# The last two steps of a graph network kernel's layer 3: products combined, weighed, normalized and stored one by one, with row additions on GpSimd

## The chip, the cores and the metric

The kernel runs on one core of a Trainium2 chip. A core has a matrix engine (TensorE, PE in the profile, with its weight loads as PEld), VectorE (DVE), ScalarE (ACT), GpSimd (POOL) and SyncE (SP, which here only issues transfers). They run at the same time, each in its own instruction order, and wait for one another by semaphores. The metric is the device time of one execution in microseconds.

## The reference

Four layers over 4096 nodes with 256 features, each followed by a residual addition and a layer normalization. Layer 0 is a masked attention with four heads, layer 1 a graph attention, and layers 2 and 3 are graph convolutions. The change concerns the end of layer 3:

```python
def _L3_gnn_ref(H, A_tilde, W):
    d_inv_sqrt = jnp.sum(A_tilde, axis=1) ** (-0.5)
    A_norm = d_inv_sqrt[:, None] * A_tilde * d_inv_sqrt[None, :]
    H_next = A_norm @ H @ W
    return jax.nn.relu(H_next)
...
# x: (4096, 256), adj: (4096, 4096)
x = _layernorm(x + _L0_gnn_ref(x, adj, adj, ...), axis=-1)
x = _layernorm(x + _L1_gnn_ref(x, adj, L1_gnn_W, L1_gnn_a), axis=-1)
x = _layernorm(x + _L2_gnn_ref(x, adj, L2_gnn_W, L2_gnn_b), axis=-1)
x = _layernorm(x + _L3_gnn_ref(x, adj, L3_gnn_W), axis=-1)
return x
```

## The kernel before, in words

Everything is float32. Layers 0 and 1 come first and are not touched. Layers 2 and 3 share one loop of 128 steps, 64 a layer (`n_all = 2 * T1`). A layer computes adj @ y, where y is x scaled by the inverse root of the row sums, in four blocks (`jb`) of output nodes. A block covers 512 nodes of the first half of the nodes and the 512 at the same place in the second half, and runs over 16 steps (`c`), each with one chunk of 128 input nodes from either half.

The 2x2 split of nodes and features lets a step use seven products in place of eight (Strassen's scheme). `sums` (L946) makes five sums and differences of the adjacency chunk on VectorE, `prepare` (L910) made those of y earlier, and `Block.product` (L959) issues product i of step t: one matmul of 128x128 with 128x512 that accumulates over the block's 16 steps in PSUM tile `m[i]`. [...]

When a block ends, `keep` (L982) copies the seven results to the SBUF tile `e`, four on ScalarE (L986) and three on VectorE (L988). `combine(h)` (L991) adds them up on VectorE into `hT`, the transposed result of half h. `rows(n)` (L1007) handles one chunk of 128 output nodes, n from 0 to 7: two matmuls with the layer's weights into `py` (L1014), for layer 3 a relu with scale on ScalarE (L1028) into a tile `relu` that has three buffers, an addition onto the residual `xc` on VectorE (L1029), and the statistics of the row (`ln_stats`, L115 and L116). `block_rstd` (L903) turns the eight variances into inverse deviations (L906 to L908), and `store(h)` (L1032) normalizes four chunks into `ob` on VectorE (`ln_apply`, L124) and sends them to `out` by one transfer of 512 KB from SP (L1037).

The order is written by hand (`tc.manual_schedule`): each engine gets its instructions in program order. For every block but the last, `at_step` (L1043) spreads these later parts over the following steps, so that they lie beside the next block's products. For the last block there is no next one: after the last step the loop breaks and everything runs in sequence, with the rows' `py` in the PSUM tiles of the products:

```python
            for h in range(2):
                blk.combine(h)
                for n in range(h * NSJ, (h + 1) * NSJ):
                    blk.rows(n, f"m{n % 7}")
            block_rstd(NJB - 1)
            for h in range(2):
                blk.store(h)
```

`load` (L935) fetches the adjacency three steps ahead on SP; `sums(t + 1)` stands ahead of the products of step t.

Of the kernel before, what the change touches and what calls it, by code (L numbers as in the profile page):

```python
# [8 lines left out]
F32 = mybir.dt.float32  # L9
BF16 = mybir.dt.bfloat16  # L10
AF = mybir.ActivationFunctionType
ALU = mybir.AluOpType
# [4 lines left out]
P = 128  # L17
N = 4096
D = 256
# [5 lines left out]
BJ = 512  # L25
# [19 lines left out]
def tile_gnn(  # L45
# [18 lines left out]
    nc = tc.nc  # L64
# [18 lines left out]
    d3 = const.tile([P, NCH], F32, name="d3")  # L83
# [8 lines left out]
    xc = keep.tile([P, NCH, D], F32, name="xc")  # L92
# [20 lines left out]
    def ln_stats(pool, row, ci):  # L113
        st = pool.tile([P, 6], F32, tag="bnst", name="bnst")
        nc.vector.bn_stats(st, row)  # L115
        nc.vector.bn_aggr(mv[:, ci, :], st)  # L116

    def ln_rstd(c0, c1):
        nc.vector.tensor_scalar(rstd[:, c0:c1], mv[:, c0:c1, 1], EPS, None, ALU.add)
        nc.scalar.activation(rstd[:, c0:c1], rstd[:, c0:c1], AF.Sqrt)  # L120
        nc.vector.reciprocal(rstd[:, c0:c1], rstd[:, c0:c1])

    def ln_apply(dst, src, ci):
        nc.vector.tensor_scalar(  # L124
            dst, src, mv[:, ci, 0:1], rstd[:, ci : ci + 1], ALU.subtract, ALU.mult
        )

# [43 lines left out]
    with ExitStack() as l0:  # L171
# [6 lines left out]
        wk = l0.enter_context(tc.tile_pool(name="l0work", bufs=1))  # L178
# [176 lines left out]
        class Pair:  # L355
# [80 lines left out]
            def sums(self):  # L436

                u = 2 * self.rows.ib + self.pr
                l2 = wk2.tile([P, 2], F32, tag="l2", name="l2")
                nc.vector.tensor_reduce(l2, self.ls, AX.X, ALU.add)  # L440
                nc.vector.reciprocal(l2, l2)

                lt = wk2.tile([P, QB], F32, tag="lt", name="lt")
                nc.vector.transpose(lt, l2.unsqueeze(1).to_broadcast([P, QB // 2, 2]))
                for j in range(2):
                    nc.gpsimd.dma_start(
                        norm[u, j, :].rearrange("(a c) -> a c", c=QB),
                        lt.rearrange("(a r) c -> a r c", r=QB)[:, j, :],
                    )
# [17 lines left out]
        rows = [Rows(ib) for ib in range(NCH)]  # L467
# [244 lines left out]
    with ExitStack() as l1:  # L712
        wk = l1.enter_context(tc.tile_pool(name="l1work", bufs=2))
# [166 lines left out]
    with ExitStack() as l2:  # L880
# [3 lines left out]
        wk = l2.enter_context(tc.tile_pool(name="l2work", bufs=3))  # L884
        ps_m = l2.enter_context(tc.tile_pool(name="l2ps_m", bufs=1, space=PSUM))

        w2_sb = big.tile([P, 2, D], F32, name="w2_sb")
# [3 lines left out]
        w3_sb = big.tile([P, 2, D], F32, name="w3_sb")  # L891
        nc.scalar.dma_start(w3_sb, w3.rearrange("(c p) e -> p c e", p=P))

        NP = NCH // 2
        NJB = N // 2 // BJ
        NSJ = BJ // P
        T1 = NJB * NP
        y = store[:, 0 : 2 * NP * D].rearrange("p (h c e) -> p h c e", h=2, c=NP)
# [4 lines left out]
        def block_rstd(jb):  # L903
            cs = slice(jb * NSJ, (jb + 1) * NSJ)
            r = rstd2[:, :, cs]
            nc.vector.tensor_scalar(r, mv2[:, :, cs, 1], EPS, None, ALU.add)  # L906
            nc.scalar.activation(r, r, AF.Sqrt)
            nc.vector.reciprocal(r, r)  # L908

        def prepare(p, layer):  # L910

            dv = d2 if layer == 0 else d3
            for h in range(2):
                ci = h * NP + p
                ln_apply(xc[:, ci, :], xc[:, ci, :], ci)
                nc.scalar.activation(
                    y[:, h, p, :], xc[:, ci, :], AF.Copy, scale=dv[:, ci : ci + 1]
                )
                if layer == 0:
                    nc.gpsimd.tensor_tensor(xc[:, ci, :], xc[:, ci, :], b2_b, ALU.add)  # L920
            s = ysum[:, p, :, :]
            nc.vector.tensor_tensor(
                s[:, 1:3, :].rearrange("p a d -> p (a d)"), y[:, 0, p, :], y[:, 1, p, :], ALU.subtract
            )
            nc.vector.tensor_tensor(
                s[:, 3:5, :], y[:, :, p, 0:P], y[:, :, p, P : 2 * P], ALU.add
            )
            nc.vector.tensor_tensor(
                s[:, 0, :], y[:, 0, p, 0:P], y[:, 1, p, P : 2 * P], ALU.add
            )  # L930
# [23 lines left out]
        class Block:  # L954
# [49 lines left out]
                    tt(o, o, e[2], ALU.add)  # L1004
                    tt(o, o, e[5], ALU.subtract)

            def rows(self, n, tag="y"):  # L1007

                h, s = divmod(n, NSJ)
                ci = h * NP + self.jb * NSJ + s  # L1010
                w = w2_sb if self.layer == 0 else w3_sb
                py = ps_m.tile([P, 512], F32, tag=tag, name="py")
                for f in range(2):
                    nc.tensor.matmul(  # L1014
                        py[:, 0:D],
                        self.hT[:, h, f, s * P : (s + 1) * P],
                        w[:, f, :],
                        start=(f == 0),
                        stop=(f == 1),
                    )  # L1020
                row = xc[:, ci, :]
                if self.layer == 0:
                    nc.vector.scalar_tensor_tensor(
                        row, py[:, 0:D], d2[:, ci : ci + 1], row, ALU.mult, ALU.add
                    )
                else:
                    r = wk.tile([P, D], F32, tag="relu", name="relu")
                    nc.scalar.activation(r, py[:, 0:D], AF.Relu, scale=d3[:, ci : ci + 1])  # L1028
                    nc.vector.tensor_tensor(row, row, r, ALU.add)  # L1029
                ln_stats(wk, row, ci)  # L1030

            def store(self, h):  # L1032
                ob = wk.tile([P, NSJ, D], F32, tag="ob", name="ob", bufs=2)
                c0 = h * NP + self.jb * NSJ
                for s in range(NSJ):
                    ln_apply(ob[:, s, :], xc[:, c0 + s, :], c0 + s)
                nc.sync.dma_start(  # L1037
                    out[c0 * P : (c0 + NSJ) * P, :].rearrange("(s p) e -> p s e", p=P), ob
                )
# [3 lines left out]
        def at_step(t, when, f, *args):  # L1043
            later.setdefault((t, when), []).append((f, args))

        def do(t, when):
            for f, args in later.pop((t, when), []):
                f(*args)

        n_all = 2 * T1  # L1050
# [3 lines left out]
        with tc.manual_schedule():  # L1054
            prepare(0, 0)
            sums(0)
            prepare(1, 0)
            blk = None
            for t in range(n_all):
                layer, tl = divmod(t, T1)  # L1060
                jb, c = divmod(tl, NP)
                if c == 0:
                    blk = Block(layer, jb)
                if t + 3 < n_all:
                    load(t + 3)
                if t + 1 < n_all:
                    sums(t + 1)
                for i in range(7):
                    blk.product(i, t)
                    if i == 2:  # L1070
                        do(t, "mid")
                del adj_t[t], adj_s[t]
                if layer == 0 and jb == 0 and c + 2 < NP:
                    prepare(c + 2, 0)
                do(t, "end")
                if c == NP - 1:
                    blk.keep()
                    if t == n_all - 1:
                        break
                    at_step(t + 1, "mid", blk.combine, 0)  # L1080
                    at_step(t + 2, "mid", blk.combine, 1)
                    for n in range(2 * NSJ):
                        at_step(t + 2 + n // 2, ("mid", "end")[n % 2], blk.rows, n)
                    at_step(t + 2 + NSJ, "mid", block_rstd, jb)
                    for s in range(NSJ):
                        p = jb * NSJ + s
                        if layer == 0:

                            free = (NJB - 1) * NP + p + NSJ + 2
                            at_step(max(t + 2 + NSJ + s, free), "end", prepare, p, 1)  # L1090
                    if layer == 1:
                        for h in range(2):
                            at_step(t + 3 + NSJ + h, "end", blk.store, h)
            for h in range(2):
                blk.combine(h)
                for n in range(h * NSJ, (h + 1) * NSJ):
                    blk.rows(n, f"m{n % 7}")
            block_rstd(NJB - 1)
            for h in range(2):
                blk.store(h)  # L1100


# [49 lines left out]
```

## Time and profile before

| | us |
|---|---|
| median of 3 runs (2745.74 to 2746.96) | 2745.95 |
| the profiled execution | 2743.03 |
| its span, first to last instruction | 2741.3 |
| last two steps start (products) | 2703.33 |
| last product ends, about | 2715.4 |
| last normalization ends, about | 2736.9 |

The profile's times count from the span's start. Two rows of the groups show what the same kind of addition takes on two engines (columns: line, engine, operation, output and inputs with shapes, count, then busy us and the mean ns of one, then idle time before it):

```profile
L1029 DVE TENSOR_TENSOR xc<-xc,relu 128x256 f32<-128x256 f32 x8 | 3.3, 409 | 4.3 <-ACT relu L1028 4.3
...
L920 POOL TENSOR_TENSOR xc<-xc,b_b 128x256 f32<-128x256 f32 x32 | 25.5, 816 | 529.1 <-ACT store L916 529.1
```

The first row is the last block's additions. The second is the only addition of this size that GpSimd does in these two layers, at the start of layer 2. A duration in such a row is from an instruction's start to its end; neighbours on one engine may overlap a little.

### The profile page before, as it was taken

The numbers are of one execution on the slowest core, as the hardware profiler recorded it, in microseconds if no ns is written. First come the engines' busy times: TensorE is split into PE (matmuls) and PEld (weight loads), VectorE is DVE, ScalarE is ACT, GpSimd is POOL, SyncE is SP. The second block draws the span as 40 slices with busy tenths as digits, with TensorE's granted clock in tenths as the row PEclk, the third lists the DMA queues.
The fourth block names the chain that finished last, engine by engine and source line by source line (L and its number), as shares of the span: only waits on it lengthen the run. The fifth ranks groups of instructions, "written<-read, shape, count | busy, mean of one in ns | idle before, by whom it ended". The sixth has DMA issues, their size and how long they took to land.

```text
span 2741.3 us, 58184 instructions
## 1 busy us (share of the span) xinstructions
PE 2688.6 (98%) x23440; PEld 1840.8 (67%) x23440; DVE 2183.8 (80%) x3995; ACT 1648.0 (60%) x2675; POOL 379.4 (14%) x660
## 2 busy tenths in 40 slices
PE   8999999999999999999979999999999999999997
PEld 5777777777777777777768888886444444444443
DVE  4899889899898989889758888885866578666565
ACT  2899999999999999999857777771100001000000
POOL 1232222232222222222200000001200000000000
PEclk9999999999999999999999999999999999999998
DMA  6444444444444444444352222203545544555552
GB/s 148 94 94 95 89 92 95 90 92 92 91 95 91 91 94 95 86 95 95 125 171 77 77 77 77 73 28 118 178 158 164 167 160 154 169 173 165 184 170 75
DMA packets 679486, 312.31 MB, mean 114 GB/s; under 512 B 553520, under 2 KB 583600, under 8 KB 679216
## 3 DMA queue, kind: packets, MB, share of 16 engines
q1 hardware_dynamic: 655776, 265.10, 38.9%
q0 software_dynamic: 21632, 42.05, 4.3%
q8 instruction: 183, 3.00, 0.5%
q10 hardware_dynamic: 1808, 1.44, 0.2%
q14 instruction: 87, 0.71, 0.1%
HBM read 262.41 MB, written 46.07 MB: 113 GB/s over the span
## 4 chain that ended last, share of the span: by engine, by line
PE 96%; DVE 2%; issue 1%; DMA 1%; ACT 1%; SPq 0%; POOL 0%; DVEq 0%; ACTq 0%; POOLq 0%
PE m L980 27%; PE po L428 18%; PE sc L371 16%; PE po L802 16%; PE ptr L410 11%; PE py L1014 2%; PE pp L340 1%; PE pq L319 1%; PE pv L232 1%; PE pk L212 1%; PE sc L139 1%; DMA xt<-in_xT 0%; SPq L262 0%; DMA rb<-norm 0%; DVE pt L416 0%
## 5 line engine op out<-in xcount | busy, mean ns | idle before, releaser
L380 DVE CUSTOM_DVE_ANT_0 z<-sc,bias 128x1024 f32<-128x1024 f32 x512 | 606.0, 1221 | 48.0 <-PE sc L371 47.9
L396 ACT ACTIVATE z<-z,nm 128x1024 f32<-128x1024 f32 x512 | 590.4, 1153 | 0.0
L418 ACT COPY pt<-ptr 128x1024 f32<-128x1024 f32 x507 | 510.5, 1007 | 78.3 <-PE ptr L410 75.2
L428 PE MATMUL po<-pt,xc 128*64 128x128 f32 x8192 | 504.1, 276 | 0.0
L371 PE MATMUL sc<-store,qT 64*128 64x512 f32 x2048 | 502.9, 604 | 0.1
L802 PE MATMUL po<-store,pt 128*128 128x257 f32 x2048 | 447.6, 380 | 12.6 <-issue 12.6
L428 PEld LDWEIGHTS po<-pt,xc 128*64 128x64 f32 x8192 | 442.1, 137 | 17.5 <-DVE pt L416 0.2
L410 PEld LDWEIGHTS ptr<-ident,z 64*128 64x128 f32 x8192 | 322.0, 138 | 178.4 <-issue 82.5
L802 PEld LDWEIGHTS po<-store,pt 128*128 128x128 f32 x2048 | 388.9, 190 | 71.1 <-issue 12.7
L980 PE MATMUL m<-asum,ysum 128*128 128x512 f32 x768 | 356.2, 593 | 6.3 <-issue 6.3
L410 PE MATMUL ptr<-ident,z 64*128 64x64 f32 x8192 | 356.6, 225 | 4.5 <-ACT pt L418 3.2
L371 PEld LDWEIGHTS sc<-store,qT 64*128 64x128 f32 x2048 | 192.7, 188 | 116.7 <-issue 109.8
L980 PEld LDWEIGHTS m<-asum,ysum 128*128 128x128 f32 x768 | 146.0, 190 | 177.9 <-issue 161.2
L980 PE MATMUL m<-asum,store 128*128 128x512 f32 x512 | 262.3, 594 | 0.0
L980 PE MATMUL m<-a,ysum 128*128 128x512 f32 x512 | 245.7, 593 | 0.0
L986 ACT COPY e<-m 128x512 f32<-128x512 f32 x32 | 18.5, 585 | 351.4 <-PE m L980 351.4
L301 POOL DMA_DIRECT2D edge<-mk x256 | 143.5, 561 | 558.7 <-ACT mk L295 544.7
L756 ACT ACTIVATE z<-z,es_q 128x1024 f32<-128x1024 f32 x128 | 146.5, 1145 | 120.8 <-DVE mx L743 114.4
L949 DVE TENSOR_TENSOR asum<-a 128x512 f32<-128x512 f32 x128 | 88.0, 688 | 164.1 <-PE m L980 164.1
L284 DVE SCALAR_TENSOR_TENSOR bias<-rt,gb,u 128x512 f32<-128x512 f32 x256 | 194.4, 759 | 9.1
L792 DVE STREAM_TRANSPOSE pt<-z 128x1024 f32<-128x1024 f32 x128 | 158.1, 1237 | 42.1 <-PE po L802 42.1
L278 DVE STREAM_TRANSPOSE rt<-raw 128x512 f32<-128x512 f32 x256 | 179.9, 703 | 0.3 <-issue 0.3
(122 smaller groups left out, 2528.8 us busy)
## 6 DMA issues: line engine op xcount, KB each, us to landing
a<-in_adjT SPq DMA_DIRECT2D x256, 512.0 KB, 5.2
raw<-in_adjT SPq DMA_DIRECT2D x512, 128.0 KB, 3.9
edge<-mk POOLq DMA_DIRECT2D x256, 128.0 KB, 2.3
mk<-edge SPq DMA_DIRECT2D x256, 128.0 KB, 2.9
xt<-in_xT SPq DMA_DIRECT2D x8, 512.0 KB, 4.6
xq<-in_xT SPq DMA_DIRECT2D x32, 128.0 KB, 3.9
xr<-in_x SPq DMA_DIRECT2D x32, 128.0 KB, 3.3
rb<-norm POOLq DMA_DIRECT2D x128, 32.0 KB, 2.4
```

The lines of the kernel that those rows point to most:

```text
L278: nc.vector.transpose(rt.rearrange("p (b r) -> p b r", r=QB), self.raw_now[:, half * nb : (half + 1) * nb, :],)
L284: nc.vector.scalar_tensor_tensor(self.bias[k][:, m0 : m0 + HT], rt, gb, u, ALU.mult, ALU.add)
L371: nc.tensor.matmul(ps[j][:, q * 512 : (q + 1) * 512], self.rows.qT[j * HD : (j + 1) * HD, self.pr, :], kT[j * HD : (j + 1) * HD, self.pr, ...
L380: nc.vector.tensor_tensor_reduce(z, ps[j], self.rows.bias[k], 1.0, NEG, ALU.add, ALU.max, self.mx[:, j, k : k + 1],)
L396: nc.scalar.activation(z, z, AF.Exp, bias=self.nm[:, j : j + 1], accum_out=self.ls[:, j, k : k + 1],)
L410: nc.tensor.transpose(pa[:, r, c, :], z[half, c * P : (c + 1) * P], ident[half, half])
L418: nc.scalar.copy(to, pa)
L428: nc.tensor.matmul(self.po[j * HD : (j + 1) * HD, 0:P], v_sb[:, ci, h * HD : (h + 1) * HD], self.pt[j][k][:, c, :], start=(ci == 0), stop= ...
L756: nc.scalar.activation(self.z[s], self.z[s], AF.Prelu, bias=self.eq[:, s : s + 1], alpha=SLOPE)
L792: nc.vector.transpose(self.pt[:, :, s, :], self.z[s].rearrange("p (b r) -> p b r", r=QB))
L802: nc.tensor.matmul(self.po[:, 0 : D + 1], self.pt[:, b, :, :].rearrange("p s i -> p (s i)"), wh[:, b, :], start=(b == 0), stop=(b == NBK - 1),
L980: nc.tensor.matmul(self.m[i], left, right, start=(c == 0), stop=(c == NP - 1))
```

## The change: the last two steps product by product

At step n_all - 2 the loop makes the sums for the last step and issues no products. At the last step it calls the new `Block.end`, which issues the products of both steps together, product 2 twice, then 4, 0, 3, 6, 1 and 5. ScalarE copies products 2, 4, 0 and 3 to SBUF as they end; products 6, 1 and 5 are read from PSUM by VectorE's additions. Half 0 of `hT` is complete after product 6, and half 1 after products 1 and 5. The weights' matmuls (`weigh`, now a method of its own) of rows 0 and 1 stand ahead of product 5, those of rows 2 and 3 behind it, then the first matmul of each of rows 4 to 7, then the second ones. Rows 0 to 3, 4 and 6 are added onto `xc` by GpSimd, rows 5 and 7 by VectorE. Each half has its own rstd, four normalizations (the last half's chunk 3 on GpSimd) and two transfers of 256 KB; the very last one is issued from ScalarE's queue. `rows` for the other blocks issues the same instructions as before.

```diff
--- before.py
+++ after.py
@@ -120,8 +120,8 @@
         nc.scalar.activation(rstd[:, c0:c1], rstd[:, c0:c1], AF.Sqrt)
         nc.vector.reciprocal(rstd[:, c0:c1], rstd[:, c0:c1])
 
-    def ln_apply(dst, src, ci):
-        nc.vector.tensor_scalar(
+    def ln_apply(dst, src, ci, engine=nc.vector):
+        engine.tensor_scalar(
             dst, src, mv[:, ci, 0:1], rstd[:, ci : ci + 1], ALU.subtract, ALU.mult
         )
 
@@ -1004,20 +1004,25 @@
                     tt(o, o, e[2], ALU.add)
                     tt(o, o, e[5], ALU.subtract)
 
-            def rows(self, n, tag="y"):
+            def weigh(self, n, py, f):
+
+                h, s = divmod(n, NSJ)
+                w = w2_sb if self.layer == 0 else w3_sb
+                nc.tensor.matmul(
+                    py[:, 0:D],
+                    self.hT[:, h, f, s * P : (s + 1) * P],
+                    w[:, f, :],
+                    start=(f == 0),
+                    stop=(f == 1),
+                )
+
+            def rows(self, n):
 
                 h, s = divmod(n, NSJ)
                 ci = h * NP + self.jb * NSJ + s
-                w = w2_sb if self.layer == 0 else w3_sb
-                py = ps_m.tile([P, 512], F32, tag=tag, name="py")
+                py = ps_m.tile([P, 512], F32, tag="y", name="py")
                 for f in range(2):
-                    nc.tensor.matmul(
-                        py[:, 0:D],
-                        self.hT[:, h, f, s * P : (s + 1) * P],
-                        w[:, f, :],
-                        start=(f == 0),
-                        stop=(f == 1),
-                    )
+                    self.weigh(n, py, f)
                 row = xc[:, ci, :]
                 if self.layer == 0:
                     nc.vector.scalar_tensor_tensor(
@@ -1028,6 +1033,88 @@
                     nc.scalar.activation(r, py[:, 0:D], AF.Relu, scale=d3[:, ci : ci + 1])
                     nc.vector.tensor_tensor(row, row, r, ALU.add)
                 ln_stats(wk, row, ci)
+
+            def end(self, t0):
+
+
+                tt = nc.vector.tensor_tensor
+                e = wk.tile([P, 7, BJ], F32, tag="e", name="e", bufs=1)
+                hT = self.hT = wk.tile([P, 2, 2, BJ], F32, tag="hT", name="hT", bufs=1)
+                m, o0, o1 = self.m, e[:, 1, :], e[:, 5, :]
+                e0, e2, e3, e4 = (e[:, i, :] for i in (0, 2, 3, 4))
+                py = {}
+
+                def products(i):
+                    for t in (t0, t0 + 1):
+                        self.product(i, t)
+                    if i in (0, 2, 3, 4):
+                        nc.scalar.copy(e[:, i, :], m[i])
+
+                def weigh(n, tag, fs=(0, 1)):
+                    if n not in py:
+                        py[n] = ps_m.tile([P, 512], F32, tag=tag, name="py")
+                    for f in fs:
+                        self.weigh(n, py[n], f)
+
+                def onto_x(n):
+                    h, s = divmod(n, NSJ)
+                    ci = h * NP + self.jb * NSJ + s
+                    r = wk.tile([P, D], F32, tag="relu", name="relu")
+                    nc.scalar.activation(r, py[n][:, 0:D], AF.Relu, scale=d3[:, ci : ci + 1])
+                    eng = nc.vector if n > NSJ and n % 2 else nc.gpsimd
+                    eng.tensor_tensor(xc[:, ci, :], xc[:, ci, :], r, ALU.add)
+
+                def stats(n):
+                    h, s = divmod(n, NSJ)
+                    ci = h * NP + self.jb * NSJ + s
+                    ln_stats(wk, xc[:, ci, :], ci)
+
+                def put(h, engines):
+                    c0 = h * NP + self.jb * NSJ
+                    ln_rstd(c0, c0 + NSJ)
+                    ob = wk.tile([P, NSJ, D], F32, tag="ob", name="ob", bufs=2)
+                    for s in (0, 1, 3, 2):
+                        ln_apply(ob[:, s, :], xc[:, c0 + s, :], c0 + s, engines[s])
+                    for s, queue in ((0, nc.sync), (2, (nc.sync, nc.scalar)[h])):
+                        queue.dma_start(
+                            out[(c0 + s) * P : (c0 + s + 2) * P, :].rearrange(
+                                "(s p) e -> p s e", p=P
+                            ),
+                            ob[:, s : s + 2, :],
+                        )
+
+                products(2)
+                products(4)
+                products(0)
+                products(3)
+                tt(hT[:, 0, 1, :], e2, e4, ALU.add)
+                tt(o0, e0, e4, ALU.subtract)
+                tt(o1, e0, e2, ALU.add)
+                tt(o0, o0, e3, ALU.subtract)
+                products(6)
+                tt(hT[:, 0, 0, :], o0, m[6], ALU.add)
+                products(1)
+                tt(hT[:, 1, 0, :], m[1], e3, ALU.subtract)
+                tt(o1, o1, m[1], ALU.subtract)
+                weigh(0, "m2")
+                weigh(1, "m4")
+                products(5)
+                tt(hT[:, 1, 1, :], o1, m[5], ALU.subtract)
+                weigh(2, "m0")
+                weigh(3, "m3")
+                for n in range(NSJ):
+                    onto_x(n)
+                    stats(n)
+                for n, tag in zip(range(NSJ, 2 * NSJ), ("m6", "m1", "m5", "y")):
+                    weigh(n, tag, (0,))
+                put(0, [nc.vector] * NSJ)
+                for n in range(NSJ, 2 * NSJ, 2):
+                    for i in range(n, n + 2):
+                        weigh(i, None, (1,))
+                        onto_x(i)
+                    stats(n)
+                    stats(n + 1)
+                put(1, [nc.vector] * (NSJ - 1) + [nc.gpsimd])
 
             def store(self, h):
                 ob = wk.tile([P, NSJ, D], F32, tag="ob", name="ob", bufs=2)
@@ -1065,6 +1152,10 @@
                     load(t + 3)
                 if t + 1 < n_all:
                     sums(t + 1)
+                if t >= n_all - 2:
+                    if t == n_all - 1:
+                        blk.end(t - 1)
+                    continue
                 for i in range(7):
                     blk.product(i, t)
                     if i == 2:
@@ -1075,8 +1166,6 @@
                 do(t, "end")
                 if c == NP - 1:
                     blk.keep()
-                    if t == n_all - 1:
-                        break
                     at_step(t + 1, "mid", blk.combine, 0)
                     at_step(t + 2, "mid", blk.combine, 1)
                     for n in range(2 * NSJ):
@@ -1091,13 +1180,6 @@
                     if layer == 1:
                         for h in range(2):
                             at_step(t + 3 + NSJ + h, "end", blk.store, h)
-            for h in range(2):
-                blk.combine(h)
-                for n in range(h * NSJ, (h + 1) * NSJ):
-                    blk.rows(n, f"m{n % 7}")
-            block_rstd(NJB - 1)
-            for h in range(2):
-                blk.store(h)
 
 
 # ---- launch: one core ----
```

## The prediction

> **What bounds the kernel now.** I read the page first: busy shares, then the chain that ended last.
>
> ```profile
> span 2741.3 us, 58184 instructions
> PE 2688.6 (98%) x23440; PEld 1840.8 (67%) x23440; DVE 2183.8 (80%) x3995; ACT 1648.0 (60%) x2675; POOL 379.4 (14%) x660
> ...
> PE 96%; DVE 2%; issue 1%; DMA 1%; ACT 1%; SPq 0%; POOL 0%; DVEq 0%; ACTq 0%; POOLq 0%
> ```
>
> TensorE carries 96% of the chain, so work moved on other engines is worth something only where the chain leaves TensorE. The edit touches the last two of 128 steps alone, so next I read the end by windows (columns: stretch, its length, then busy us of PE, PEld, DVE, ACT and POOL with counts, granted clock, DMA share, GB/s).
>
> ```profile
> 2703.30:2715.40 12.10, 12.10 (x29) 5.13 (x27) 5.06 (x7) 1.76 (x3) 0.00 (x0) 1.00 0.00 0
> 2715.40:2717.60 2.20, 0.11 (x1) 0.00 (x0) 1.99 (x4) 0.59 (x1) 0.00 (x0) 1.00 0.00 0
> 2717.60:2721.60 4.00, 3.89 (x16) 2.87 (x16) 2.50 (x8) 1.47 (x4) 0.00 (x0) 1.00 0.00 0
> 2721.60:2724.30 2.70, 0.00 (x0) 0.02 (x1) 2.56 (x9) 0.42 (x1) 0.00 (x0) 0.90 0.00 0
> 2724.30:2731.70 7.40, 6.60 (x16) 4.59 (x16) 4.26 (x10) 1.42 (x3) 0.00 (x0) 0.57 0.00 0
> 2731.70:2737.00 5.30, 0.00 (x0) 0.00 (x0) 4.67 (x16) 0.68 (x2) 0.00 (x0) 0.72 0.09 31
> 2737.00:2741.30 4.30, 0.00 (x0) 0.00 (x0) 0.00 (x0) 0.00 (x0) 0.00 (x0) 0.50 0.61 206
> ```
>
> The first row is the last two steps: TensorE full. After 2715.4 come 25.9 us in which TensorE has 10.5 us of work (eight output rows) and waits twice for VectorE; GpSimd does nothing. The second four rows run at a granted clock of 0.57. The chain in order of time says who is late (start, length, what):
>
> ```profile
> 2715.30 0.69 DVE hT L996
> ...
> 2716.88 0.70 DVE hT L998
> ...
> 2717.62 1.31 PE py L1014 x4
> ...
> 2725.53 0.70 DVE hT L1005
> 2726.23 0.04 issue
> 2726.28 2.94 PE py L1014 x6
> ...
> 2731.37 0.44 DVE xc L1029
> 2731.81 0.02 issue
> 2731.83 0.44 DVE bnst L115
> ...
> 2733.50 0.18 DVE rstd L906
> ...
> 2734.92 1.93 DVE ob L124 x6
> ```
>
> Combination of half 0 on VectorE, matmuls, row work on VectorE, and only then the combination of half 1 (L1005 is queued behind the rows of half 0), its matmuls, rows, one rstd, eight normalizations and the stores. It is a serial chain with two alternating engines.
>
> **What the Trainium skill says.** "TensorE: Matmul & The Clock Gate", Part 1, has two clocks, full when the array has been busy and half after an idle window of about 3.4 us. The trace agrees in direction: 1.00 until 2721.6, then 0.50 to 0.59 after an idle of 2.7 us that followed one of 2.2 us. "GPSIMD Engine Reference", section 3, puts a two-input elementwise add at about twice VectorE's time; here an add of 128x256 takes 0.81 us on GpSimd (L920) and 0.41 on VectorE (L1029), the same ratio. Its section 1 says GpSimd shares SBUF interfaces with VectorE, and section 2.1 that a freshly loaded kernel's first call may cost about 6 us; neither shows in this trace (the adds of L335 all take 0.73 to 0.76 us, the first one included). "DMA: Bandwidth & Descriptors", in its two cost components, gives a fixed part of about 2 us, mostly the write's receipt; the stores of L1037 land 3.0 to 3.5 us after issue, with 512 KB each.
>
> **The change part by part.** Product i of the last two steps takes a slot of 0.858 us (in the timeline P1 of the last step starts at 2710.20, P0 at 2709.34; seven make the 6.01 us of a step). The last two steps start at 2703.33.
>
> *Products.* The same 14, in the order 2, 4, 0, 3, 6, 1, 5, both steps of each together; 12.01 us of TensorE as before. New risk: P4 of the last step now comes fourth, at 2705.91, and needs the second sum of that step, which L950 ends at 2705.36 (start 2704.14, 1.22 long). In time by 0.55, cost 0; had the sums come 1 us later, TensorE would lose 0.45. The slots end: P2 2705.05, P4 2706.77, P0 2708.48, P3 2710.20, P6 2711.92, P1 2713.63.
>
> *Combination.* ScalarE copies four products (0.59 each) instead of four of seven; three are read by VectorE straight from PSUM and their three copies (0.69 each) go. The PSUM-source adds aren't in the trace: bounds 0.69 (both the copy from PSUM L988 and the SBUF add L998 take that) and 1.4 (add after copy); I take 0.69. Half 0 is ready 2711.92 + 0.20 (L988 starts 0.20 after its product's slot) + 0.69 = 2712.8, before TensorE wants it at 2713.63. So the waits of 2.2 and 2.7 us go. A row is four passes of 0.215, 0.86 in all (the relus of L1028 start 0.86 apart). Rows 0, 1 to 2715.35; P5 to 2717.07; rows 2, 3 to 2718.79; the four first halves of rows 4 to 7 to 2720.51 (half 1's first part is ready by 2714.6, its second by 2717.96); the four second halves end 2720.94, 2721.37, 2721.80, 2722.23. TensorE never idles, so I keep the full clock: it is done at 2722.2 instead of 2731.7.
>
> *Rows 0 to 3.* Relu 0.47 on ScalarE, starting 0.19 after the row; the add on GpSimd 0.81, with 0.08 from ScalarE to GpSimd (L916 to L920) and about 0.05 from GpSimd to VectorE (L111 starts 0.04 after its ident). The adds end at 2716.0, 2716.9, 2719.5, 2720.34. VectorE does statistics at 0.57 per row (0.47 + 0.10 from start to start); the last starts at 2720.41, ends 2721.06. Then rstd of four: 0.18, 0.21, 0.20 with gaps, as L906 to L908, to 2721.75; four applies at 0.32 to 2723.16. ScalarE's root stands ahead of relu 4, which was ready at 2721.13 and starts at 2721.53: 0.4 late. The relus behind it wait too, and VectorE's add of row 5 behind the four applies anyway.
>
> *Rows 4 to 7.* Relus 2721.53 to 2723.47; GpSimd adds rows 4 and 6, ended 2722.9 and 2723.9; VectorE starts row 5's add at 2723.07 and then has two adds (0.34 from start to start) and four statistics (0.57): 2726.09. Rstd to 2726.77, three applies from 2726.81 end at 2727.87. The fourth apply is on GpSimd, which no row shows: bounds 0.29 (the select of 128x128) and 0.81 (the add of this size); even 0.81 ends at 2727.7, hidden under VectorE's.
>
> *Stores.* Four of 256 KB instead of two of 512. The first two are issued by 2723.2 and have landed long before the end. The last two go from SP at 2727.6 and from ScalarE's queue at 2727.9 (0.38 on SP, 0.44 to 0.49 as ScalarE's queue shows at the start; no work is queued behind either). Before, data flowed from 0.9 after the first issue (2735.59, then 2736.5), at about 345 GB/s; 512 KB instead of 1 MB take 1.5 instead of 3.0 us: from 2728.5 to 2730.0. Landing came 0.6 after the data, the span's end 1.1 after that: 2731.75. So the part after the last apply shrinks from 4.45 to 3.9, and the sum is 2741.3 - 2731.75 = 9.55 us: 9.0 from the compute chain (2736.85 to 2727.87), 0.55 from the stores.
>
> *The rest.* Moving two matmuls into a helper changes no instruction earlier on; all earlier steps keep their order and waits. The profiled execution took 2743.03 us, 1.7 over its span; the median of the runs is 2745.95. I take the difference off the median: 2736.4 us.
>
> **Rivals.**
> A: GpSimd and VectorE get in each other's way. For: the skill's shared interface; against: the adds of L920 beside VectorE's work take 0.72 to 0.91, hardly more than L335's 0.74. If the three GpSimd instructions beside half 1's VectorE work (0.81 each) fully shut it out, plus 0.15 more at four handoffs: 3.0 us back, 2739.4.
> B: GpSimd's first scalar-tensor operation costs a first call of 6 us (an estimate from the skill's figure). Its apply would then end at 2733.6, 5.7 late: 2742.1, no change that can be told. Against: L335's first call.
> C, slower: the adds on GpSimd become the chain. Six adds of X in series give a last apply near 2720.0 + 6X; at X = 2.9 us nothing is gained, and from X = 3.8 it is slower by 5.5 us, 2751.5. The trace's longest is 0.91, and only semaphore work of GpSimd that the trace doesn't show could make that.
> D: more than the sum, if GpSimd's adds and the handoffs are quicker or the stores of 256 KB land earlier: 2735, at most 1.5 us.
> That the change doesn't do what it says would show as TensorE waiting in the products; the instruction order has the waits as computed, so I give it nothing of its own.
>
> **How the numbers follow.** Forecast 0.76, A 0.14, B 0.03, C 0.02, D 0.05. Range: the forecast's own unknowns (0.7 for PSUM reads that delay nothing while TensorE is behind, 0.5 for stores, 0.6 for the runs' own spread of 1.2 us, 0.5 for handoffs) give about 1.5 either way; stretched half way into A: 2734.9 to 2738.8. About 0.2%, 5.5 us, is what a measurement can tell from no change. Faster is all but B, C and the far end of A: 0.94; same 0.04; slower 0.02.
>
> **What would show it.** After: no TensorE gap over 0.2 us from 2703 to 2722, clock 1.00 there; GpSimd adds of about 0.8; a gap of 0.4 ahead of relu 4; the last apply near 2727.9; span near 2731.8. Wrong if P4 waits for the sums, if the statistics wait for GpSimd over 1 us each, or if GpSimd's apply ends last.

## The result, and the profile after

| us | before | after |
|---|---|---|
| median of 7 runs | 2745.46 (2741.6 to 2746.96) | 2735.45 (2734.41 to 2738.59) |
| the profiled execution | 2743.03 | 2734.41 |
| its span | 2741.3 | 2732.6 |
| first product of the last two steps to the span's end | 37.97 | 29.32 |

The change makes the kernel 0.3% faster: ratio 0.997, with a 95% interval of 0.9958 to 0.9981. The last row, called the stretch from here on, is the better gauge. It starts where the last two steps' products start (0.20 us ahead of the last L949, which waits for the product before them). Everything earlier is unchanged, and its time varies by several microseconds from run to run, while the stretch repeated within 0.07 us when the changed kernel ran a second time (29.39; a span is given to 0.1 us).

The windows of after first (columns as before: stretch, length, busy us of PE, PEld, DVE, ACT and POOL with counts, granted clock, DMA share, GB/s):

```profile
2703.30:2722.40 19.10, 19.07 (x61) 11.21 (x59) 11.62 (x23) 5.42 (x12) 3.45 (x5) 1.00 0.00 0
```

```profile
2722.40:2728.70 6.30, 0.00 (x0) 0.00 (x0) 5.69 (x18) 0.79 (x3) 2.26 (x3) 0.88 0.25 83
2728.70:2732.60 3.90, 0.00 (x0) 0.00 (x0) 0.00 (x0) 0.00 (x0) 0.12 (x1) 0.50 0.40 134
```

TensorE is busy for 19.07 of 19.10 us at full clock and has done all eight rows by 2722.4. What is left after it is 6.3 us in which VectorE is busy for 5.69, and the end with the stores. Before, 25.9 us followed the last product; now 15.5 follow product 5's end at 2717.1, and two of the eight rows are through the array by then.

The chain that ended last, in order of time (start, length, what):

```profile
2717.19 1.74 PE py L1011 x8
...
2719.57 0.74 POOL xc L1065
...
2720.32 0.44 DVE bnst L115
...
2721.00 0.18 DVE rstd L119
...
2721.32 0.47 ACT relu L1063
...
2721.85 0.72 POOL xc L1065
...
2723.39 3.98 issue
2727.36 1.46 POOLq L1230
```

The back and forth between TensorE and VectorE is gone: the chain leaves TensorE once, at 2718.9, and not again. Its end needs care. It is followed back from GpSimd, whose normalization ended last, and the 3.98 us of "issue" are GpSimd waiting for VectorE's rstd, a dependence that this view doesn't follow. The busy time of VectorE in the windows is the better witness for the part up to the last normalizations. The last piece, L1230 in GpSimd's queue, is the kernel's end; more of it below.

The timeline of after shows where VectorE and GpSimd meet (start, length, engine, line, operation, output and inputs, count, idle time before it and what ended it):

```profile
2720.32 0.43 DVE L115 BATCH_NORM_STATS2 bnst<-xc 128x6 f32<-128x256 f32 x1 [0.22 <-POOL xc L1065]
...
2721.32 1.19 ACT L1063 ACTIVATE relu<-py,d 128x256 f32<-128x256 f32 x3
...
2721.66 2.20 DVE L124 TENSOR_SCALAR ob<-xc,mv,rstd 128x256 f32<-128x256 f32 x4
2721.85 1.53 POOL L1065 TENSOR_TENSOR xc<-xc,relu 128x256 f32<-128x256 f32 x2 [1.56 <-ACT relu L1063]
...
2727.36 1.22 DVE L124 TENSOR_SCALAR ob<-xc,mv,rstd 128x256 f32<-128x256 f32 x3
2727.43 1.39 POOL L124 TENSOR_SCALAR ob<-xc,mv,rstd 128x256 f32<-128x256 f32 x1 [4.04 <-DVE rstd L121]
```

Statistics wait at most 0.46 us for GpSimd's additions. But half 0's four normalizations take 2.20 us and lie beside two additions on GpSimd. Before, eight took 2.67:

```profile
2734.18 2.67 DVE L124 TENSOR_SCALAR ob<-xc,mv,rstd 128x256 f32<-128x256 f32 x8
```

The instructions on tile `ob` give the spread of VectorE's seven (ns, least, median and most):

```profile
L124 DVE TENSOR_SCALAR ob<-xc,mv,rstd x7: 400/413/817, 2721.7 to 2728.2; 128x256 f32<-128x256 f32 x7
```

At the end GpSimd's single normalization takes 1.39 us and ends at 2728.82, 0.24 behind VectorE's three. The stores of that end, from the transfers' view (queue, size, us to landing):

```profile
out_x<-ob SPq DMA_DIRECT2D x1, 256.0 KB, 2.2
out_x<-ob ACTq DMA_DIRECT2D x1, 256.0 KB, 2.3
```

They land in 2.2 to 2.3 us instead of 3.0 to 3.5 with 512 KB, the last one at about 2731.2 (issued at 2728.85). But it is not the stores that end this kernel. At its end, L1230, GpSimd's queue has `DRAIN` instructions (count, ns least, median and most, first and last start):

```profile
L1230 POOLq DRAIN  x3: 40/93/4500, 2727.4 to 2732.4; - x3
```

The longest starts at 2727.36, beside the normalization, and ends at 2731.86. That is 3.04 us after the normalization's end and later than the last landing, and the span ends 0.8 us after it. In all 13 traces of this case this DRAIN ends 3.04 us after GpSimd's last operation; before, GpSimd had been idle since 1980 and nothing waited for it. From the last normalization to the span's end it is 3.78 us (2732.6 - 2728.82), before 4.45.

### The profile page after: what moved, and what is told of

The parts are those of the page before. It is cut to its first block, busy times and chain, and to the rows that moved or that the text cites. A ratio compares the mean times of both kernels' runs of the same rounds, so it can differ in the third digit from the quotient of the medians.

```text
span 2732.6 us, 58196 instructions
## 1 busy us (share of the span) xinstructions
PE 2684.7 (98%) x23440; PEld 1840.2 (67%) x23440; DVE 2179.9 (80%) x3987; ACT 1647.5 (60%) x2676; POOL 385.3 (14%) x667
## 4 chain that ended last, share of the span: by engine, by line
PE 95%; DVE 1%; DMA 1%; issue 1%; ACT 1%; SPq 0%; POOL 0%; POOLq 0%; ACTq 0%; DVEq 0%
PE m L980 28%; PE po L428 18%; PE sc L371 17%; PE po L802 16%; PE ptr L410 11%; PE py L1011 2%; PE pp L340 1%; PE pq L319 1%; PE pv L232 1%; PE pk L212 1%; DMA mk<-edge 0%; PE sc L139 0%; DMA bqk_sb<-in_bqk 0%; DVE pt L416 0%; DMA xt<-in_xT 0%
## 5 line engine op out<-in xcount | busy, mean ns | idle before, releaser
L949 DVE TENSOR_TENSOR asum<-a 128x512 f32<-128x512 f32 x128 | 88.1, 688 | 164.2 <-PE m L980 164.2
L980 PEld LDWEIGHTS m<-asum,store 128*128 128x128 f32 x512 | 97.6, 191 | 122.9 <-issue 120.8
```

Source lines behind the costliest of these rows:

```text
L980: nc.tensor.matmul(self.m[i], left, right, start=(c == 0), stop=(c == NP - 1))
```

## The experiments

All are measured by the stretch of one profiled execution each. "Last normalization" counts from the stretch's start.

| | last normalization ends | stretch | against after |
|---|---|---|---|
| before | 33.5 | 37.97 | +8.65 |
| after | 25.54 | 29.32 | |
| combinations together, else before (e3) | 28.81 | 33.22 | +3.90 |
| all additions on VectorE (e1) | 26.54 | 30.35 | +1.03 |
| rows 4 to 7 added on VectorE (e10) | 25.40 | 29.20 | -0.12 |
| chunk 3 on VectorE (e2) | 25.45 | 28.84 | -0.48 |
| one rstd, stores last (e4) | 25.31 | 29.73 | +0.41 |
| step by step (e5) | 26.69 | 30.56 | +1.24 |
| half 0 normalized on GpSimd (e7) | 25.87 | 29.66 | +0.34 |
| half 0 normalized on ScalarE (e6) | 24.94 | 28.72 | -0.60 |
| ... and chunk 3 on ScalarE (e8) | 24.61 | 28.34 | -0.98 |
| ... and started earlier (e9) | 23.85 | 27.58 | -1.74 |
| after again | 25.53 | 29.39 | +0.07 |

**Where the gain lies: only the combinations put together.** To the kernel before:

```diff
             for h in range(2):
                 blk.combine(h)
+            for h in range(2):
                 for n in range(h * NSJ, (h + 1) * NSJ):
```

> The kernel before with one edit: half 1's combination stands ahead of half 0's rows on VectorE, so that it doesn't queue behind them. Nothing on GpSimd, products, rstd and stores as before. From the first product of the last two steps to the span's end, before 37.97 us: T (TensorE's second wait and the half clock after it are half of the gain): no wait ahead of row 4, granted clock 1.00 to row 7, half 1 ready at 17.6 us, VectorE has rows from there: 8 x 0.98, rstd 0.7, eight normalizations 2.7, then 4.45: 33.4, that is 4.5 us faster. Rival (only the wait itself of 2.7 us goes, the clock falls all the same): 35.3.

```profile
2719.10:2726.50 7.40, 7.33 (x32) 5.91 (x32) 7.06 (x19) 3.31 (x7) 0.00 (x0) 1.00 0.00 0
```

This is its window over all eight rows: TensorE runs through, at clock 1.00, where before it had the waits and 0.57. The stretch is 33.22, as the theory had it (33.4) and not the rival's 35.3. One moved line brings 4.75 of the 8.65 us; in whole runs 0.9983 of before, interval 0.9977 to 0.999. The half clock came and went with the wait that the queue order on VectorE made. Of the other 3.90 us up to after, the next runs take parts away one at a time; their values don't add up to it. Reading products 6, 1 and 5 straight from PSUM, and rows 0 and 1 ahead of product 5, were not measured alone.

**Whether the additions on GpSimd help.** In `onto_x`:

```diff
-                    eng = nc.vector if n > NSJ and n % 2 else nc.gpsimd
+                    eng = nc.vector
```

> All eight row additions of the last block on VectorE; GpSimd keeps only the last half's chunk 3. Measured from the first product of the last two steps to the span's end (before 37.97 us, after 29.32). Theory T (GpSimd and VectorE hinder each other in the normalizations, so GpSimd's additions save next to nothing): half 0's four normalizations fall from 2.20 us back to about 1.4; VectorE has six more additions, of which about 1.7 us reach the end, less 0.8 from the normalizations: 30.2. Rival R (the additions on GpSimd are the gain, and the slow normalizations have another cause, such as the stores): normalizations stay at 2.2 us and the end comes 2.3 us later, 31.6.

The same four normalizations in its timeline:

```profile
2724.66 1.38 DVE L124 TENSOR_SCALAR ob<-xc,mv,rstd 128x256 f32<-128x256 f32 x4
```

1.38 instead of 2.20: with GpSimd idle they are as quick as before, and the stretch of 30.35 is the theory's (30.2), not the rival's 31.6. So GpSimd's six additions are worth 1.03 us in all. Only 0.8 of it is on VectorE, whose last normalizations start that much later; the other 0.2 is GpSimd's own normalization, which starts 0.15 us behind VectorE's instead of 0.07 and takes 1.53 us instead of 1.39. The next run asks which additions count.

```diff
-                    eng = nc.vector if n > NSJ and n % 2 else nc.gpsimd
+                    eng = nc.vector if n >= NSJ else nc.gpsimd
```

> GpSimd adds rows 0 to 3 only; rows 4 to 7 are added by VectorE; chunk 3 of the last half stays on GpSimd. Theory (GpSimd's two additions beside half 0's normalizations cost VectorE there 0.8 us and save it two additions of 0.35): normalizations back at 1.4 us, first product to end 29.2, no difference to after's 29.32 within 0.2. Rival (GpSimd's additions in half 1 pay, the stretched normalizations are spare time): 0.7 us longer, 30.0.

```profile
2727.78 1.38 DVE L124 TENSOR_SCALAR ob<-xc,mv,rstd 128x256 f32<-128x256 f32 x4
```

Here too the four normalizations are back at 1.38 us. The stretch is 29.20: the two additions of half 1 on GpSimd are worth nothing (-0.12). What VectorE saves in additions it loses in normalizations beside them. The whole gain comes from rows 0 to 3 (1.15 us, e1 less e10). On GpSimd, rows 2 and 3 lie beside statistics, and rows 0 and 1 lie in a wait of VectorE for product 5, which after's timeline has as

```profile
2717.23 0.69 DVE L1102 TENSOR_TENSOR hT<-e,m 128x512 f32<-128x512 f32 x1 [2.16 <-PE m L980]
```

The relus of rows 0 and 1 are done at 2715.2 and 2716.0. In e1 their additions stand behind L1102 in VectorE's queue; two of 0.4 us would fit into the 2.16 us ahead of it (an estimate from these figures). So a part of the 1.15 us may be due to the order and not to GpSimd. No run tests that.

**GpSimd's normalization.** First, VectorE in its place:

```diff
-                put(1, [nc.vector] * (NSJ - 1) + [nc.gpsimd])
+                put(1, [nc.vector] * NSJ)
```

> The last half's chunk 3 normalized on VectorE instead of GpSimd. T: the four take 1.4 us on VectorE from the same start and end where GpSimd's single one of 1.39 us ended: the stretch from first product to end stays at 29.3 us within 0.15. R (GpSimd saves VectorE one normalization): 0.3 us longer, 29.6.

Neither value: 28.84, lower than both. The last normalization ends 0.09 earlier, near the theory; the other 0.39 lie between it and the end (3.39 us instead of 3.78). The cause is GpSimd's DRAIN. GpSimd's last operation is now an addition that ends at 2727.06, and the DRAIN is over 3.04 us later, at 2730.1, before the last two stores are issued:

```profile
L1230 POOLq DRAIN  x3: 40/102/3873, 2726.2 to 2735.5; - x3
```

```profile
2732.44 0.40 ACTq L1079 DMA_DIRECT2D out_x<-ob  x1
```

Now the last store sets the end: it lands 2.3 us after its issue, and the span ends 1.1 us later. In the seven traces in which GpSimd normalizes last, the end comes 3.8 to 3.9 us after that normalization. In e8 and e9 GpSimd normalizes nothing, and their 3.73 us have another reason: the last store is issued only 0.37 us behind the one before it (0.65 in e2) and takes 2.5 to 2.6 us to land. From the landing on they need 1.1 us like e2. So the last chunk on GpSimd cost the changed kernel 0.48 us.

Then a measurement of GpSimd's operation, with half 0's four on it and rows 4 to 7 added on VectorE:

> A measurement of GpSimd's normalization: half 0's four on GpSimd, where VectorE runs additions and statistics beside them, and rows 4 to 7 added on VectorE. T (1.39 us came from VectorE's normalizations beside it): those beside statistics and additions take 0.6 to 0.9 us. Rival (GpSimd's normalization is slow by itself): all take 1.3 us or more. Time from first product to end: not later than after by more than 0.3, since VectorE gives up 2.2 us and takes 0.7.

Its groups by line (busy us, mean ns, then idle):

```profile
L124 POOL TENSOR_SCALAR ob<-xc,mv,rstd 128x256 f32<-128x256 f32 x5 | 7.3, 1477 | 1.5 <-DVE rstd L121 1.5
...
L124 DVE TENSOR_SCALAR ob<-xc,mv,rstd 128x256 f32<-128x256 f32 x3 | 1.1, 434 | 0.0
```

And the five by tile `ob` (ns, least, median and most):

```profile
L124 POOL TENSOR_SCALAR ob<-xc,mv,rstd x5: 1214/1512/1735, 2724.2 to 2730.3; 128x256 f32<-128x256 f32 x5
```

The theory fell: 0.6 to 0.9 us occurs nowhere. The rival is right in the main, though two of the five stay under its 1.3 us. The last one starts at 2730.3, when VectorE has finished (2729.78), and takes 1.21 us; the first two, beside additions and statistics, take over 1.7. So GpSimd's normalization is slow by itself, three times VectorE's 0.41, although it has a single tensor input, and VectorE's work beside it makes it slower. "GPSIMD Engine Reference" of the Trainium skill, section 4.1, calls one-input work on GpSimd roughly line-rate; for this operation with its two scalars per partition the trace says otherwise (1.21 us at least, where GpSimd's two-input addition takes 0.73), and the trace decides.

**Stores of half 0 ahead, or all at the end.** `put(0, ...)` is left out and `put(1, ...)` replaced:

```diff
-                put(1, [nc.vector] * (NSJ - 1) + [nc.gpsimd])
+                block_rstd(NJB - 1)
+                for h in range(2):
+                    self.store(h)
```

> One rstd for both halves, all eight normalizations on VectorE and two stores of 512 KB at the very end, the rest as after. T: with nothing running on GpSimd beside them the eight take 2.7 us; the last ends about 0.4 us earlier than after's, but 1 MB is stored last, 4.45 us instead of 3.8: first product to end 29.5 us. R (taking half 0's normalizations and stores ahead is worth their time): 1.4 us or more longer, 30.7 to 31.5.

```profile
2729.11 2.67 DVE L124 TENSOR_SCALAR ob<-xc,mv,rstd 128x256 f32<-128x256 f32 x8
```

29.73. Eight undisturbed normalizations at the end stop 0.23 us earlier than after's, and behind them it takes 0.64 more (4.42 instead of 3.78). Against after the split of the halves is worth 0.41 us. But this edit also takes the last normalization off GpSimd, as e2 does, and against e2 the split is worth 0.89: 1 MB of stores at the end costs 1.03 more than half of it (4.42 and 3.39 us), and the last normalization is only 0.14 earlier.

**Pairing the two steps.**

```diff
+                for i in (2, 4, 0, 3, 6, 1, 5):
+                    self.product(i, t0)
+
                 def products(i):
-                    for t in (t0, t0 + 1):
-                        self.product(i, t)
+                    self.product(i, t0 + 1)
```

> The products of the step before the last are issued first, then those of the last step, both in the order 2, 4, 0, 3, 6, 1, 5; the rest as after. T (what counts is that each product of the last step is used as it ends, not that two steps are paired): half 0 is ready about 0.3 us before TensorE wants it, rows 2 to 7 keep their times: 29.3 us within 0.2. Rival (the pairing gives VectorE the time it needs): TensorE waits 0.9 us or more for half 0 and the end comes as much later, 30.2 or more.

```profile
2717.48 0.89 PE L1011 MATMUL py<-w_sb,hT 128*128 128x256 f32 x3 [0.91 <-DVE hT L1097]
```

The theory fell: TensorE waits 0.91 us for half 0 ahead of row 0, and the stretch is 1.24 longer. With one step the products end 0.86 us apart, and VectorE's five additions up to half 0 take 0.6 to 0.8 each, so VectorE is late. I had also left out that rows 0 and 1 stand ahead of product 5. The pairing spaces the products 1.72 us apart, which is what hides the combination.

**VectorE's queue after the last matmul.** Half 0's normalizations go to ScalarE (scale rstd, bias -mean x rstd, the bias from one small product `nm` on VectorE), issued behind the relus of rows 4 to 7:

```diff
-                        ln_apply(ob[:, s, :], xc[:, c0 + s, :], c0 + s, engines[s])
+                        nc.scalar.activation(
+                            ob[:, s, :], xc[:, c0 + s, :], AF.Identity,
+                            bias=nm[:, s : s + 1], scale=rstd[:, c0 + s : c0 + s + 1],
+                        )
```

> Half 0's four normalizations on ScalarE, behind the relus of rows 4 to 7; one small product of mean and rstd more on VectorE; chunk 3 of the last half stays on GpSimd. T (after row 7's matmuls VectorE's queue sets the end, 5.7 busy us of 6.3): the 2.2 us of normalizations leave VectorE, 0.2 come, and VectorE then waits about 0.3 for a relu: 1.5 to 1.8 us shorter than after, 27.5 to 27.8 us from first product to end. Rival (the chain of relus and GpSimd additions of rows 4 to 7 sets it): at most 0.5 shorter, 28.8.

28.72, only 0.60 less than after: nearer the rival's value, but its timeline shows another reason:

```profile
2724.24 0.39 DVE L1065 TENSOR_TENSOR xc<-xc,relu 128x256 f32<-128x256 f32 x1
2724.55 0.15 DVE L1081 SCALAR_TENSOR_TENSOR nm<-mv,rstd 128x4 f32<-128x4 f32 x1
...
2724.74 2.07 ACT L1086 ACTIVATE ob<-xc,nm,rstd 128x256 f32<-128x256 f32 x4 [1.27 <-DVE nm L1081]
...
2726.94 0.18 DVE L121 RECIPROCAL rstd<-rstd 128x4 f32<-128x4 f32 x1 [0.95 <-ACT rstd L120]
```

`nm` stood behind row 7's addition, so ScalarE waited 1.27 us for it, and the last half's root then queued behind four normalizations while VectorE waited 0.95. The next run had chunk 3 on ScalarE as well, with the same fault:

> As e6, and the last half's chunk 3 on ScalarE too, so that nothing of GpSimd runs beside VectorE's normalizations. T: the last three on VectorE take 1.06 instead of 1.22 us, ScalarE's one 0.5: 0.2 shorter than e6, about 27.4 us from first product to end, 1.9 less than after; in whole runs some 0.4% below before. Rival as for e6: 28.6 or more.

28.34, 0.38 less than e6; whole runs 0.9965 of before (0.9953 to 0.9977). The last store lands only 0.1 us earlier than in e6 (27.2 and 27.3 us after the stretch's start); the rest is GpSimd's DRAIN, which no longer ends last. Then `nm` was put right behind half 0's rstd:

> As e8, but the product of mean and rstd that ScalarE's normalizations need stands right behind half 0's rstd on VectorE instead of behind the addition of row 7, so that they start 1.2 us earlier, right after the relus. Theory (e6 and e8 fell short because the last half's root, ready at 22.3 us after the first product, queued 0.7 us behind half 0's normalizations on ScalarE): the root starts without a wait and the whole stretch from first product to end is 0.7 us shorter than e8's 28.34: 27.6. Rival (the relus and GpSimd's additions hold rows 4 to 7): it stays at 28.2 to 28.4. Whole runs: 0.35 to 0.4% below before; against after, 1.7 us of stretch, near what runs can tell.

```profile
2725.11 2.06 ACT L1087 ACTIVATE ob<-xc,nm,rstd 128x256 f32<-128x256 f32 x4
...
2727.69 0.20 ACT L120 ACTIVATE rstd<-rstd 128x4 f32<-128x4 f32 x1 [0.52 <-DVE rstd L119]
```

Now ScalarE waits for VectorE ahead of the root, not the other way round, and the stretch is 27.58, as the theory said. It beats both kernels in the stretch, by 1.74 us against after; 0.3 to 0.4 of this is the end without GpSimd's DRAIN. Beside it the changed kernel ran again:

> The changed kernel again beside e9, on the same chip: first product to end 29.3 us within 0.1, and its whole runs 0.3 to 0.37% below before; e9 lower than it by 1 to 2 us in the median if the stretch alone decides.

In whole runs e9 has a median of 2734.37 us (ratio 0.9958, 0.9946 to 0.9971) and after 2735.83 (0.9963, 0.995 to 0.9977): the right way, but the intervals overlap, so only the stretch shows it.

## Why the prediction was right

**The time.** Forecast 2736.4 us, measured 2735.45, inside the range. The sum's own quantity, the span, was forecast at 2731.75 and is 2732.6: 8.7 us gained of 9.55. The median gained 10.0, within what runs differ by. So the median came out 0.95 us better than forecast and the span 0.85 worse; that the median lies so near is partly luck.

**TensorE.** Right in every slot: P4 of the last step was not held up, half 0's last addition starts at 2712.07 (forecast 2712.1), the rows are done at 2722.4 (2722.2), clock 1.00. The PSUM-source additions take 0.69 us, the lower of the two bounds. That the waits and the half clock go together with VectorE's order is shown by e3. One reading of before was a little off. The clock was full for 2 us longer than the 2721.6 of the prediction:

```profile
2722.60:2723.60 1.00, 0.00 (x0) 0.00 (x0) 0.93 (x5) 0.00 (x0) 0.00 (x0) 1.00 0.00 0
2723.60:2724.60 1.00, 0.28 (x1) 0.32 (x2) 1.00 (x2) 0.00 (x0) 0.00 (x0) 0.59 0.00 0
```

It fell after about 2.3 us without a matmul, less than the idle window that the prediction cites, and not in the first wait of 2.1 us. These runs don't show what decides.

**Rows 0 to 3.** Right: 0.73 us for an addition on GpSimd (forecast 0.81), the last statistics from 2720.32 (2720.41). The root delayed relu 4 by about 0.2 us instead of 0.4.

**Half 0's normalizations.** The first mis-sized term: about 1.4 us forecast, 2.20 measured. This is rival A's mechanism, at a quarter of its price: 0.8 us, not 3.0. e1 and e10 show that GpSimd's additions cause it, since 1.38 comes back without them. The prediction had set the term to nothing from the additions of L920, that is from GpSimd's side alone; what VectorE loses beside them it had not looked up. The skill's sentence on shared interfaces ("GPSIMD Engine Reference", section 1) limits the contention to VectorE instructions in a two-port mode or with two inputs in SBUF. The runs agree for two kinds: statistics beside GpSimd's additions stay at 0.40 to 0.43 us, and of VectorE's two additions in e6 the one beside a GpSimd addition takes 0.68 us and the other 0.39. The normalization has one tensor input, and its longest takes 0.82 us instead of 0.41; in which mode it runs, no view shows.

```profile
2722.24 1.59 POOL L1065 TENSOR_TENSOR xc<-xc,relu 128x256 f32<-128x256 f32 x2 [1.56 <-ACT relu L1063]
2722.56 0.68 DVE L1065 TENSOR_TENSOR xc<-xc,relu 128x256 f32<-128x256 f32 x1 [0.55 <-ACT relu L1063]
...
2724.24 0.39 DVE L1065 TENSOR_TENSOR xc<-xc,relu 128x256 f32<-128x256 f32 x1
```

**The fourth normalization on GpSimd.** The second mis-sized term: bounds of 0.29 and 0.81, measured 1.39. Both rows I took were of other operations. It was not hidden: it ended 0.24 us behind VectorE's three, which took 1.22 instead of 1.06. That it ends last is one of the signs that the prediction lists for being wrong, and here the mechanism was wrong: this chunk is on the path to the end. The two terms and this 0.16 explain 0.82 + 0.16 + 0.24 = 1.22; smaller terms gave 0.3 back before the last normalization (2728.82 against 2727.87), and the part after it 0.1.

**Stores.** Right in size only by luck: 3.78 us instead of the 3.9 forecast, but what ended last was GpSimd's DRAIN, for which the sum had no term. The stores alone would have ended the span at about 2732.3, 3.5 us after the last normalization (an estimate: the landing at 2731.2 and the 1.1 us that e2 needs from there). The reading of before's end was off too: its last landing is at 2740.1, 0.35 us after the data and 1.2 ahead of the span's end, not 0.6 and 1.1.

**The other rivals.** B did not occur: GpSimd's normalization in e1, its first operation in 748 us, took 1.53 us, 0.14 more than in after, and not 6. C did not occur either. Of D the quicker additions are there (0.73 us for 0.81), but the gain in the stretch was less than the sum, not more.

## What to carry to other kernels

Look at the end of a kernel as a schedule of its own: when one engine's queue order makes another wait, reordering alone can bring most of the gain, here 4.75 us of 8.65 from one moved line, with TensorE at full clock throughout. Give GpSimd work that lies beside statistics or a wait of VectorE, not beside normalizations or additions on it, and price each operation by a row of that very operation. Don't give GpSimd the last piece of work: in these runs the kernel's end then waited for GpSimd after all stores had landed. An idle third engine, here ScalarE, is the better helper, provided that nothing urgent queues behind what it is given.

## What the runs showed of the hardware

At the kernel's end GpSimd's queue stays in a DRAIN until 3.04 us after GpSimd's last operation, in all 13 traces. In the seven in which GpSimd normalizes last, this is what the span's end waits for.

A normalization of 128x256 with two scalars per partition takes GpSimd 1.21 us with VectorE idle (e7) and up to 1.74 us beside VectorE's work, where its two-input addition of the same size takes 0.73 in after's first four rows; a cheaper-looking operation is the dearer one.

The spread of whole runs has more than one place. Layer 0's first L340 is at 133.2 us in the profiled execution of before and at 138.3 in that of e10, whose code up to there is the same. With that, e10's run of 2740.4 us is the longest of the variants of after, although its stretch is shorter than after's by 0.12. In the other traces the first L340 is at 133.2 to 134.8, and from there to the stretch's start they differ by another 4 us.
